# Inverse window transform of a fused attention and filter kernel: half of the third tile's columns are computed on the other half of the partitions, in a fourth accumulator bank

## The chip, the cores and the metric

The kernel runs on one core of one Trainium2 chip. The metric is device time in microseconds (us) of one execution. The time before is the median of three executions. One execution was also taken with the hardware profiler, and all durations below come from that one.

The engines are called by the profile's names. PE is the matrix engine (TensorE), with its weight loads shown apart as PEld. DVE is VectorE, ACT is ScalarE, POOL is GpSimd and SP issues most of the transfers. An accumulator bank (PSUM) holds 512 fp32 numbers on each of 128 partitions. PE writes only there, and ACT or DVE copy from there to the working memory (SBUF).

## The reference, cut to what matters

The input is 8 images of 384 channels and 64 x 64 pixels, all fp32. There are two layers, each added to its input:

```
x = x + windowed attention(group norm(x))
x = x + second layer(group norm(x))

second layer:
  t  = w_in @ x                                  # 384 channels to 384, each pixel alone
  tf = rfft2 of every 8 x 8 window of t          # "P = 8"
  t  = irfft2(tf * fft_filter)                   # back to pixels
  t  = 3 x 3 depthwise convolution of t          # zero padding at the image's edge
  g  = gelu(t[:192], exact) * t[192:]
  out = w_out @ g                                # 192 channels to 384
```

The change lies in the line with `irfft2`. A real 8 x 8 window has 64 numbers, and the kernel does its transform as a product with a 64 x 64 matrix.

## The kernel before, in words

An image is cut into 8 strips of 8 rows. A strip has 8 windows of 64 pixels, so 512 pixels, and 384 channels, so three tiles of 128 channels x 512 pixels. The second layer's hidden channels are permuted so that tile 0 and tile 1 go together into the gate (`gelu(tile 0) * tile 1`), while tile 2 holds the last 64 channels of both halves.

The work is a list of pieces. Each piece is put at a place in time with `at(place, piece, ...)` (lines 848 to 947), and the pieces are then traced in the order of their places (line 953). PE's instructions stay in exactly that order (`keep_in_program_order`, line 62). A scheduler orders the instructions of the other engines by its own estimate of when their inputs are ready. The second layer of one image runs in the same stretch of time as the attention layer of the next, so that seven eighths of the kernel is one steady mixture; the second layer of the last image runs alone.

Two units of places make a strip. In the second unit of each strip the pieces that matter here come on PE in this order, with the names that the profile shows:

- `v_tile` (line 490): the attention's values for the next image's strip, accumulated in `pvv` twice; ACT copies each to `v` at line 503. Between the two stands `turn` (line 551, tile `pT`), a transpose of attention weights.
- `back` (line 684): the inverse transform. The filtered spectrum is in two tiles `t2`, each for four windows, whose 128 partitions are two halves of 64 frequencies; which half holds which channels is told by the index `h`. Each matmul takes 64 channels of one window (`t2` as the stationary matrix, 64 x 64) and the 64 x 64 basis `inv`, and leaves 64 channels x 64 pixels in an accumulator `pz`. The row half of the PE array is `h`, the column half is the half of the partitions of `pz` that is written.
- `apply` (line 562, tile `pA`): attention weights times values, 32 matmuls of 64 x 64 that go round all four quarters of the PE array.
- `scores` (line 505, tile `pS`): the next strip's attention scores, also 64 x 64 blocks.
- `finish` (line 810): the last product of an older strip of the second layer. It first multiplies 64 rows of `g1` into two banks `pw` and then into the double bank `pw2`, and then does dense 128 x 128 matmuls with `zz` (the profile's `pw<-zz`).
- `qk_tile`, `project` and `mix` follow, which are dense 128 x 128 matmuls.

On ACT, `inner` (line 702) copies a tile from `pz` to a bordered image tile `z` of 10 x 66, from which DVE later does the convolution. `back` calls it for tiles 0 and 2; `borders` (line 713) calls it for tile 1 and then copies border rows between neighbouring strips (lines 718 and 719). `put` (line 587) copies `pA` into `o` with four copies on ACT at lines 602 to 605, or two at line 599, and POOL then issues transfers from `o` to `oT` (line 615). The square at line 376 (`sq<-y`) and the first tap at line 779 come next on ACT.

There are eight accumulator banks. Four single banks take turns under the tag `gemm` (`ps`, `bufs=4`): each new tile takes the bank of the tile four allocations earlier and waits until that one has been read. The other four banks are two double banks under the tag `att` (line 55), which `pT`, `pA`, `pS` and `pw2` take in turn. So `pw2` takes the double bank of `pA` and can be written only when `put` has copied `pA`.

In `back` the first group of matmuls fills tiles 0 and 2, with four matmuls for each window, one for each quarter of the PE array. The second group fills tile 1, with two matmuls for each window on two opposite quarters. An fp32 matmul is two passes in the profile, so the groups have 64 and 32 passes.

The table `EMPTY` (line 29) tells how many empty instructions are spread over PE's dense matmuls ahead of each stretch of small ones. `small_tiles` marks those stretches.

Of the kernel before, what the change touches and what calls it, by code (L numbers as in the profile page):

```python
# [8 lines left out]
AF = mybir.ActivationFunctionType  # L9
# [3 lines left out]
P = 128  # L13
KC = 3
C = 384
WS = 8
SW = 64
ST = WS * SW
NS = SW // WS
# [6 lines left out]
C_ID, C_ONES, C_GRP, C_FWD, C_INV, C_MASK = 0, 128, 256, 384, 512, 640  # L26
C_PICK = C_MASK + 3 * 64
N_CONST = C_PICK + 2
EMPTY = (129, 0, 0, 96, 52, 0, 0, 98, 11, 124, 11, 124, 3, 124, 11, 124, 11, 45, 43, 124, 52, 123, 11, 124,
# [9 lines left out]
def block_kernel(ctx: ExitStack, tc: tile.TileContext, out, x, consts, fsel, wqk, wv, bqk, bv,  # L39
                 wp, bp, lng, lnb, rpb1, rpb2, w_in, w_dw, w_out, filt):  # L40
    nc = tc.nc
# [8 lines left out]
    def psum(name):  # L50
        return ps.tile([P, ST], F32, tag="gemm", name=name)
# [9 lines left out]
    def matmul(*args, **kw):  # L61
        tc.keep_in_program_order(nc.tensor.matmul(*args, **kw))  # L62

        n = min(fetched["empty"], fetched["share"])
        for _ in range(n):
            tc.keep_in_program_order(nc.tensor.nop(hint="empty"))
        fetched["empty"] -= n
# [28 lines left out]
    inv = cst[:, C_INV:C_INV + P]  # L96
# [71 lines left out]
    for br, tab in ((0, rpb1), (1, rpb2)):  # L168
        raw = sb.tile([P, 2, 64], F32, tag="t2", bufs=3, name=f"rpb_raw{br}")
        raw_bias.append(raw)  # L170
        for h in range(4):
            half = slice(h % 2 * 64, h % 2 * 64 + 64)
# [117 lines left out]
    def by_window(t):  # L290

        return t.rearrange("p (w r c) -> p w r c", w=NS, r=WS)
# [10 lines left out]
    xs, ys, y2s, qks, vs, os_, ots, x1s, zs = ({} for _ in range(9))  # L303
# [380 lines left out]
    def back(b, s):  # L684

        t2 = [zs.pop((b, s, "t2", j)) for j in range(2)]
        pz = [psum(f"pz_{b}_{s}_{m}") for m in (0, 2, 1)]
        pz = {0: pz[0], 2: pz[1], 1: pz[2]}

        for parts in (((0, 0, 0, 0), (2, 1, 1, 128), (0, 1, 0, 64), (2, 0, 1, 64)),  # L690
                      ((1, 0, 0, 128), (1, 1, 1, 0))):
            for i in range(4):
                for p in range(2):
                    for m, half, h, c in parts:
                        rows = slice(h * 64, (h + 1) * 64)
                        matmul(pz[m][half * 64:(half + 1) * 64, (2 * i + p) * 64:(2 * i + p + 1) * 64],
                               t2[i // 2][rows, p, i % 2, c:c + 64], inv[rows, rows], start=True, stop=True)
        zs[b, s, "pz"] = pz
        for m in (0, 2):
            inner(b, s, m)  # L700

    def inner(b, s, m):
        z = z_bufs[zs["count"] % len(z_bufs)]
        zs["count"] += 1
        if s == 0:
            nc.gpsimd.memset(z[:, 0, 1:SW + 1], 0.0)
        if s == NS - 1:
            nc.gpsimd.memset(z[:, WS + 1, 1:SW + 1], 0.0)
        nc.scalar.activation(z[:, 1:9, 1:SW + 1].rearrange("p r (w c) -> p w r c", c=WS),
                             by_window(zs[b, s, "pz"][m]), AF.Copy)  # L710
        zs[b, s, m] = z

    def borders(b, s):

        inner(b, s, 1)
        for m in (0, 2, 1) if s else ():
            above, z = zs[b, s - 1, m], zs[b, s, m]
            after_out(nc.scalar.copy(above[:, WS + 1, 1:SW + 1], z[:, 1, 1:SW + 1]))  # L718
            after_out(nc.scalar.copy(z[:, 0, 1:SW + 1], above[:, WS, 1:SW + 1]))
# [128 lines left out]
    for b in range(B):  # L848
# [25 lines left out]
        for s in range(NS):  # L874
# [18 lines left out]
            for br in range(2):  # L893
                w = u + br
# [27 lines left out]
        for s in range(NS):  # L922
            u = first + 2 + 2 * s
            at(u - 0.84, load, b, s, "mix")
            at(u + 0.02, normal_x1, b, s)
            for i in range(4):
                at(u + (0.28, 0.45, 0.60, 0.78)[i], mix, b, s, i)
            for j in range(2):
                at(u + (0.995, 1.02)[j], transform, b, s, j)
            if b < B - 1:  # L930
                at(u + 1.985, small_tiles, u + 2)
            at(u + 1.99, back, b, s)
            at(u + 2.08 if b < B - 1 or s < NS - 1 else u + 1.991, borders, b, s)

            for n, m in enumerate((0, 2, 1)):
                for tap in range(1, 6):
                    at(u + (2.62, 3.10, 3.5)[n] + 0.05 * tap + (0.4 if n == 2 and tap > 3 else 0), conv, b, s, m, tap)
                for tap in range(6, 9):
                    at(u + 4.2 + 0.25 * (n * 3 + tap - 6) / 9, conv, b, s, m, tap)
            if (b, s) in on_pool:  # L940
                for place, taps in ((2.45, (0, 1)), (2.8, (2, 3)), (3.15, (4, 5)), (4.15, (6, 7)), (4.3, (8,))):
                    at(u + place, pool_taps, b, s, taps)
            if (b, s) in on_pe:
                at(u + 2.3, conv_taps, b, s)
            at(u + 5.16, load, b, s, "finish")
            at(u + 4.5, gate, b, s)
            at(u + 6.10, finish, b, s)
# [5 lines left out]
    order = [p[2:] for p in sorted(plan, key=lambda p: p[:2])]  # L953
    dense, empty, counts = [], [0] * len(order), list(EMPTY)
    for i, (piece, args) in enumerate(order):
# [116 lines left out]
```

## Time and profile before

| what | value |
|---|---|
| median of 3 executions | 3534.49 us (3533.04 to 3534.71) |
| the profiled execution | 3528.99 us, span of its instructions 3526.8 us |
| mean granted PE clock | 0.992 |
| PE busy | 3450.3 us (98%) |
| DVE busy | 3062.2 us (87%) |
| ACT busy | 2535.8 us (72%) |
| POOL busy | 1055.3 us (30%) |
| `pz` matmuls | 6144 passes, 146.7 us busy |
| copies of `pz` to `z` (line 709) | 192 of 128x512, 656 ns each |

The profiled execution took 5.5 us (0.16%) less than the median of the three others. Its span is 2.2 us shorter than its own time. A matmul's row shows 218 ns for a pass of 64 columns though a new one begins every few ns, because matmuls overlap; the chain of waits counts that overlap only once. In rows of the timeline, equal instructions that follow each other are merged: `x3` after a duration means that three instructions took that long together.

### The profile page before, as it was taken

The page shows a single profiled execution, that of the slowest core. Times are in us where ns is not written, and L with a number is a line of the kernel's source. Part 1 is how long each engine was busy: PE and PEld are TensorE (multiplying, and loading weights), DVE is VectorE, ACT ScalarE, POOL GpSimd, SP SyncE. Part 2 cuts the span into 40 slices and gives each one's busy share as a digit, 9 for nine tenths or more (in the row PEclk, how much of TensorE's full clock was granted, in tenths as well). Part 3 has the DMA queues.
Part 4 walks back from the last instruction along what each step waited for, and adds up shares of the span by engine and source line. Part 5 has one row for each costly group of instructions (what it writes and reads, how often), then busy time and mean ns, then how long its engine had stood idle before and what let it go on. Part 6 is the DMA issues. An engine that isn't in the chain of part 4 may idle for free.

```text
span 3526.8 us, 93350 instructions
## 1 busy us (share of the span) xinstructions
PE 3450.3 (98%) x36454; PEld 2192.9 (62%) x36454; DVE 3062.2 (87%) x4330; ACT 2535.8 (72%) x4069; POOL 1055.3 (30%) x1688
## 2 busy tenths in 40 slices
PE   7999999999999999999999999999999999999888
PEld 5666666666666666666666666666666666666554
DVE  5676589889998899998999889998899988987987
ACT  5877777768777687776777767777777767776574
POOL 6433222323222232222233223232232223222244
PEclk8999999999999999999999999999999999999999
DMA  4343234323343334333344324433234333323432
GB/s 135 117 128 100 88 119 138 107 101 133 130 148 108 117 107 153 120 121 109 119 136 140 119 89 141 138 116 133 101 118 156 113 107 109 108 99 104 160 109 81
DMA packets 176101, 421.13 MB, mean 119 GB/s; under 512 B 26656, under 2 KB 29243, under 8 KB 175688
## 3 DMA queue, kind: packets, MB, share of 16 engines
q1 hardware_dynamic: 138832, 364.25, 29.6%
q0 software_dynamic: 36416, 50.65, 5.1%
q8 instruction: 316, 5.18, 0.6%
q14 instruction: 97, 0.79, 0.1%
q10 hardware_dynamic: 440, 0.27, 0.0%
HBM read 263.92 MB, written 100.79 MB: 103 GB/s over the span
## 4 chain that ended last, share of the span: by engine, by line
PE 87%; DVE 8%; ACT 2%; issue 1%; DMA 1%; POOL 0%; SPq 0%; ACTq 0%; POOLq 0%; DVEq 0%
PE pq L62 26%; PE pr L62 14%; PE pvv L62 13%; PE pt L62 11%; PE pw L62 6%; PE pA L62 3%; PE pz L62 3%; PE pT L70 3%; PE pS L62 3%; DVE zz L785 2%; PE pf L62 2%; DVE acc L785 1%; PE ln L62 1%; DVE t L681 1%; ACT tap L753 1%
## 5 line engine op out<-in xcount | busy, mean ns | idle before, releaser
L785 DVE SCALAR_TENSOR_TENSOR zz<-z,dw_sb,zz 128x512 f32<-128x512 f32 x1331 | 1026.5, 797 | 10.8
L62 PE MATMUL pq<-y,wqk_sb 128*128 128x512 f32 x2160 | 989.4, 597 | 0.9 <-ACT kcd L470 0.7
L615 POOL DMA_DIRECT2D oT<-o x960 | 480.2, 508 | 963.4 <-ACT z L718 431.2
L62 PEld LDWEIGHTS pq<-y,wqk_sb 128*128 128x128 f32 x2160 | 403.1, 190 | 448.0 <-issue 407.3
L62 PE MATMUL pt<-wi_sb,xn 128*128 128x384 f32 x1536 | 535.1, 487 | 3.0 <-ACT xn L654 3.0
L62 PE MATMUL pr<-oT,wp_sb 128*128 128x512 f32 x1152 | 523.9, 593 | 1.6 <-DMA oT<-o 1.6
L62 PE MATMUL pvv<-wv_sb,y 128*128 128x192 f32 x2880 | 507.4, 326 | 0.0
L62 PEld LDWEIGHTS pvv<-wv_sb,y 128*128 128x128 f32 x2880 | 471.7, 190 | 48.6 <-issue 33.7
L62 PEld LDWEIGHTS pt<-wi_sb,xn 128*128 128x128 f32 x1536 | 290.9, 191 | 232.8 <-issue 74.1
L452 POOL COPY y<-y 128x384 f32<-128x384 f32 x112 | 86.0, 768 | 1108.0 <-PE pvv L62 643.7
L62 PEld LDWEIGHTS pr<-oT,wp_sb 128*128 128x128 f32 x1152 | 217.5, 190 | 263.7 <-issue 246.3
L470 ACT ACTIVATE kcd<-pq,bqk_sb 32x512 f32<-32x512 f32 x512 | 348.4, 680 | 9.1
L470 ACT ACTIVATE qab<-pq,bq_sb,cst 96x512 f32<-96x512 f32 (+1 forms) x256 | 197.7, 772 | 181.1 <-PE pq L62 178.7
L503 ACT COPY v<-pvv 128x384 f32<-128x384 f32 x256 | 121.4, 474 | 191.5 <-PE pvv L62 190.0
L470 ACT ACTIVATE kab<-pq,bqk_sb 96x512 f32<-96x512 f32 (+1 forms) x256 | 174.1, 680 | 90.4 <-PE pq L62 86.1
L470 ACT ACTIVATE qcd<-pq,bq_sb,cst 96x512 f32<-96x512 f32 (+1 forms) x256 | 197.4, 771 | 33.5 <-PE pq L62 27.7
L382 POOL TENSOR_TENSOR sq<-sq 128x512 f32<-128x512 f32 x122 | 201.4, 1651 | 5.8
L537 DVE TENSOR_TENSOR e<-e,mx 128x1024 f32<-128x1024 f32 x128 | 199.3, 1557 | 3.9
L530 DVE TENSOR_TENSOR e<-pS,bias 128x512 f32<-128x512 f32 (+2 forms) x200 | 108.1, 547 | 93.9 <-PE pS L62 93.9
L547 DVE TENSOR_REDUCE rc<-e 128x16 f32<-128x1024 f32 x128 | 155.1, 1211 | 35.2 <-ACT e L542 35.1
L62 PE MATMUL pw<-zz,wo_sb 128*128 128x512 f32 x496 | 182.2, 509 | 0.0
L625 DVE SCALAR_TENSOR_TENSOR x_add<-pr,vec,x_add 128x512 f32<-128x512 f32 x192 | 142.6, 743 | 38.9 <-PE pr L62 38.2
(166 smaller groups left out, 5376.3 us busy)
## 6 DMA issues: line engine op xcount, KB each, us to landing
x_add<-in_x_dram SPq DMA_DIRECT2D x64, 768.0 KB
x1d<-x_add SPq DMA_DIRECT2D x64, 768.0 KB
x_finish<-x1d SPq DMA_DIRECT2D x64, 768.0 KB
out_dram<-x_finish SPq DMA_DIRECT2D x64, 768.0 KB
x_norm<-in_x_dram SPq DMA_DIRECT2D x61, 768.0 KB
x_stats<-in_x_dram SPq DMA_DIRECT2D x56, 768.0 KB
x_mix<-x1d SPq DMA_DIRECT2D x56, 768.0 KB
oT<-o POOLq DMA_DIRECT2D x192, 96.0 KB, 3.7
```

The source lines that it names most:

```text
L62: tc.keep_in_program_order(nc.tensor.matmul(*args, **kw))
L70: tc.keep_in_program_order(nc.tensor.transpose(*args, **kw))
L382: nc.gpsimd.tensor_tensor(sq[:, 0, :], sq[:, 0, :], sq[:, k, :], ALU.add)
L452: nc.gpsimd.tensor_copy(dst[:, :, :, :, 0:4], src[:, :, :, :, 4:8])
L470: return nc.scalar.activation(dst[to:to + n], pq[of:of + n], AF.Identity, bias=bias[of:of + n], scale=scale)
L503: nc.scalar.copy(v[:, 384 * g:384 * (g + 1)], pvv[:, 0:384])
L530: nc.vector.tensor_tensor(e5[:, odd, :, a:z, :], pS[:, odd, :, a:z, :], bias_t[br, kind, odd].unsqueeze(2).to_broadcast([P, 2, z - a, 64]) ...
L537: zs["soft"] = nc.vector.tensor_tensor(e, e, mx.unsqueeze(2).to_broadcast([P, 2 * NS, 64]), ALU.subtract)
L547: nc.vector.tensor_reduce(rc, e, AX.X, ALU.add)
L615: nc.gpsimd.dma_start(out=oT[to % P:to % P + z - a, to // P, rows], in_=o[row + a:row + z, h // 2, of:of + n])
L625: after_softmax(nc.vector.scalar_tensor_tensor(t[:, m, :], pr, bp_sb[:, m:m + 1], t[:, m, :], ALU.add, ALU.add))
L785: i = nc.vector.scalar_tensor_tensor(acc.rearrange("p (r c) -> p r c", c=SW), z[:, dy:dy + 8, dx:dx + SW], dw_sb[:, m, TAPS[tap]:TAPS[tap] ...
```

## The change

`back` asks for a fourth bank, `pz_turned`. Tile 1 is now made in four windows' worth of steps instead of eight. In each step, the two matmuls as before make one of the first four windows in the bank of tile 1, and two more matmuls, on the two other quarters of the PE array, make one of the last four windows in the bank `turned`. Because those quarters have row and column halves crossed, the channels of the last four windows lie on the wrong half of the partitions. The number of matmuls stays the same.

`inner` for tile 1 then makes three copies on ACT in place of one: 128 partitions x 256 pixels from the bank of tile 1, and two of 64 partitions x 256 pixels from the bank `turned`, each going to the other half of the partitions. Tiles 0 and 2 are copied as before. One number in `EMPTY` goes from 98 to 96.

```diff
-        pz = [psum(f"pz_{b}_{s}_{m}") for m in (0, 2, 1)]
-        pz = {0: pz[0], 2: pz[1], 1: pz[2]}
+        pz = {m: psum(f"pz_{b}_{s}_{m}") for m in (0, 2, 1, "turned")}
 
         for parts in (((0, 0, 0, 0), (2, 1, 1, 128), (0, 1, 0, 64), (2, 0, 1, 64)),
-                      ((1, 0, 0, 128), (1, 1, 1, 0))):
-            for i in range(4):
-                for p in range(2):
-                    for m, half, h, c in parts:
-                        rows = slice(h * 64, (h + 1) * 64)
-                        matmul(pz[m][half * 64:(half + 1) * 64, (2 * i + p) * 64:(2 * i + p + 1) * 64],
-                               t2[i // 2][rows, p, i % 2, c:c + 64], inv[rows, rows], start=True, stop=True)
+                      ((1, 0, 0, 128), (1, 1, 1, 0), ("turned", 1, 0, 128), ("turned", 0, 1, 0))):
+            for w in range(NS if parts[0][0] == 0 else NS // 2):
+                for m, half, h, c in parts:
+                    rows, to = slice(h * 64, (h + 1) * 64), w + (NS // 2 if m == "turned" else 0)
+                    matmul(pz[m][half * 64:(half + 1) * 64, to * 64:(to + 1) * 64],
+                           t2[to // 4][rows, to % 2, to // 2 % 2, c:c + 64], inv[rows, rows], start=True, stop=True)
...
-        nc.scalar.activation(z[:, 1:9, 1:SW + 1].rearrange("p r (w c) -> p w r c", c=WS),
-                             by_window(zs[b, s, "pz"][m]), AF.Copy)
+        whole, half = slice(0, P), SW // 2
+        for m_, to, of, w in ((m, whole, whole, 0),) if m != 1 else (
+                (1, whole, whole, 0), ("turned", slice(0, 64), slice(64, P), 1), ("turned", slice(64, P), slice(0, 64), 1)):
+            cols = slice(1 + w * half, 1 + half + w * half) if m == 1 else slice(1, SW + 1)
+            tok = slice(w * ST // 2, (w + 1) * ST // 2) if m == 1 else slice(0, ST)
+            nc.scalar.activation(z[to, 1:9, cols].rearrange("p r (w c) -> p w r c", c=WS),
+                                 zs[b, s, "pz"][m_][of, tok].rearrange("p (w r c) -> p w r c", r=WS, c=WS), AF.Copy)
```

More of the change, by code (lines that the diff above doesn't have):

```diff
@@ L28 @@
 N_CONST = C_PICK + 2
-EMPTY = (129, 0, 0, 96, 52, 0, 0, 98, 11, 124, 11, 124, 3, 124, 11, 124, 11, 45, 43, 124, 52, 123, 11, 124,
+EMPTY = (129, 0, 0, 96, 52, 0, 0, 96, 11, 124, 11, 124, 3, 124, 11, 124, 11, 45, 43, 124, 52, 123, 11, 124,
          11, 124, 11, 124, 3, 124, 11, 124, 11, 45, 43, 124, 52, 123, 11, 124, 11, 124, 11, 124, 3, 124, 11, 124,
```

## The prediction

> **What bounds the kernel now.** I read the page first, its busy shares and its chain.
>
> ```profile
> PE 3450.3 (98%) x36454; PEld 2192.9 (62%) x36454; DVE 3062.2 (87%) x4330; ACT 2535.8 (72%) x4069; POOL 1055.3 (30%) x1688
> ...
> PE 87%; DVE 8%; ACT 2%; issue 1%; DMA 1%; POOL 0%; SPq 0%; ACTq 0%; POOLq 0%; DVEq 0%
> ```
>
> PE sets the time nearly everywhere, so time saved on PE counts unless PE then waits. The chain around one regular inverse transform (strip 4 of image 2, at 1492.85 us) shows what it costs. Columns: start, us, what.
>
> ```profile
> 1492.92 1.95 PE pz L62 x94
> ...
> 1494.93 0.93 PE pA L62 x61
> 1495.86 0.94 PE pS L62 x49
> 1496.79 4.07 PE pw L62 x20
> ```
>
> The 96 passes of `pz` take 1.95 us, while `pA`, 64 passes on all four quarters, takes about 0.93 us. The starts of single matmuls in the trace agree: a step begins every 58 ns, with four passes in the first group and two in the second. So each group is 16 steps, 0.93 us.
>
> Next I asked whom PE waits for: first its weight loads, then its matmuls (total us, times, longest).
>
> ```profile
> PEld pw L62 <- ACT o L605: 40.4, 51, 2.7
> ```
>
> ```profile
> PE pw L62 <- ACT o L605: 10.7, 10, 1.8
> ```
>
> In 51 of 56 strips the last thing that `pw2`'s weights wait for is ACT's last copy of `pA`. Only ten times does this stop PE itself, since the `pw` matmuls before it still run. The rows below show how near it is: the ACT timeline of the regular strip, then its weight loads.
>
> ```profile
> 1494.06 1.72 ACT L709 ACTIVATE z<-pz 128x512 f32<-128x512 f32 x3 [0.62 <-PE pz L62]
> 1495.99 0.59 ACT L602 COPY o<-pA 128x512 f32<-128x512 f32 x1 [0.21 <-PE pA L62]
> 1496.47 0.49 ACT L603 COPY o<-pA 128x384 f32<-128x384 f32 x1
> 1496.84 0.23 ACT L604 COPY o<-pA 128x64 f32<-128x64 f32 x1
> 1496.94 0.24 ACT L605 COPY o<-pA 128x64 f32<-128x64 f32 x1
> ```
>
> ```profile
> 1497.24 0.39 PEld L62 LDWEIGHTS pw<-g,wo_sb 64*64 64x64 f32 x8 [0.47 <-ACT o L605]
> 1498.02 0.30 PEld L62 LDWEIGHTS pw<-zz,wo_sb 128*128 128x128 f32 x2 [0.39 <-issue]
> ```
>
> ACT ends L605 at 1497.18, the weights go at 1497.24, and the dense `pw<-zz` begins 0.84 us after L605. In strip 7 of the same image, PE did stop:
>
> ```profile
> 1663.70 0.64 ACT L709 ACTIVATE z<-pz 128x512 f32<-128x512 f32 x1
> 1664.22 0.56 ACT L602 COPY o<-pA 128x512 f32<-128x512 f32 x1
> ...
> 1665.15 0.23 ACT L605 COPY o<-pA 128x64 f32<-128x64 f32 x1
> ```
>
> ```profile
> 1665.43 0.66 PE L62 MATMUL pw<-g,wo_sb 64*64 64x256 f32 x8 [0.85 <-ACT o L605]
> 1666.03 1.55 PE L62 MATMUL pw<-zz,wo_sb 128*128 128x512 f32 x3
> ```
>
> There `pw<-zz` comes 1666.03 - 1665.38 = 0.65 us after L605. In a regular strip, then, PE can arrive at most 0.84 - 0.65 = 0.19 us earlier before ACT's `put` holds it.
>
> **Saved on PE.** The second group's 16 steps become 8, because four quarters work at once as in the first group: 8 x 58 ns = 0.47 us for each of 64 strips, 29.9 us in all. The number of matmuls stays.
>
> **Added on ACT.** One copy of 128x512 becomes three 256 wide. The three merged copies took 1.72 us, one takes 0.656, so they start (1.72 - 0.66) / 2 = 0.53 us apart. The step by width is (0.48 - 0.10) / (512 - 64) = 0.85 ns per element, from the starts of L602 to L605. A 256-wide copy thus takes 0.53 - 256 x 0.85 ns = 0.31 us, start to start; three take 0.93, or +0.40 us a strip. No row shows one with crossed partitions. The bounds are 0.10 us (the 64-wide copy) and 0.53 (the 512-wide); worked through the steps below they give -19 and +35 us in all. I take 0.31, since the 64-, 384- and 512-wide rows lie on one line. A half of the partitions saves nothing: the Gelu rows are 629 ns with 64 partitions and 630 with 128.
>
> **The path in a regular strip.** `pz` of tile 0 is ready as before, so tile 1's copies start as before, at 1494.06 + 2 x 0.53 = 1495.12. The pieces end at 1495.12 + 0.93 = 1496.05. PE ends `pA` 0.47 us earlier, at about 1495.4, so `put` now waits for ACT instead of PE: it starts at 1496.05 against 1495.99. L605 ends at 1497.24, `pw<-zz` starts at 1497.89 against 1498.02. Of 0.47 us saved only about 0.12 arrives. About 36 strips are like this (strips 1 to 6 of most images): -4.3 us.
>
> **Where ACT is already the bound.** In the first strip of images 1 to 6 the normalisation copies of the next strip (L654) push `pz`'s copies back; in the last strip of images 0 to 5 three of them stand before tile 1's copy; and in two strips of image 6 the tap matrices (L732) do. PE waits for L605 there, so +0.40 us each goes on the path: 14 x 0.40 = +5.6 us.
>
> **The added wait.** The fourth bank was `v_tile`'s second one, so the crossed matmuls wait for its copy at L503, and `apply`, `scores` and `pw` are queued behind them. In a regular strip L503 ends 0.59 us after `pz` begins and the crossed matmuls come at 0.93, so this is hidden with 0.34 us to spare. Without that cover every us of a late L503 would stop PE. It is late in the first strips (2.63 us after the start in image 0), where ACT's queue hides it again, but image 0 has no `finish` yet, so there the second group ends 2.68 + 0.45 = 3.13 instead of 1.87: +1.3 us, once. In last strips the bank is that of the deviation at L283 (ready 2.05 us after the start, with a table load): PE stops about 1.1 us, inside the wait for L605 and a gap of 1.0 us at `pA` that it already has.
>
> **The rest.** Strip 1 of image 0, without `finish`, keeps its 0.47 us: -0.5. In the last image PE waits for DVE (17.8 us at `pz`); the tile is ready 0.47 us earlier and copied 0.40 later: 0, within 1 us either way. Behind the copies on ACT stand the border rows, L376, L779 and POOL's transfers to `oT`, all about 0.06 us later in a regular strip; PE waited for `oT` once, 1.6 us. With that cover gone, 0.06 x 56 is 3.4 us. No queue of SP or POOL changes. Two empty instructions fewer: 0; misplaced ones would show as "issue" at small matmuls, where PE now loses 5.9 us in all.
>
> **The sum.** -4.3 + 5.6 + 1.3 - 0.5 = +2.1 us. The profiled execution was 3528.99 us and would become 3531.1; the median of the runs lies 5.5 higher, so 3534.5 + 2.1 = 3536.6 us.
>
> **A rule against this change.** The row is PE's wait for L605, 51 times. The Trainium skill's page "TensorEngine Tiling (Array Packing)", section "PSUM Bottleneck", says that tiling quickens the matrix engine but not the emptying of the accumulators, whose copy may become the bottleneck. Taken at its word nothing saved on PE arrives, and the sum would lose its two negative terms, +6.9 us; the rows leave 0.12 us a strip.
>
> **The rivals.** *The saving arrives* (faster). ACT's order is the scheduler's, which put tile 1's copy ahead of `put` though it stands behind it in the program. If `put` went ahead of the turned copies, it would start at 1495.5, and L605 would no longer hold PE: 36 x -0.47 = -17 us, or -30 if all 64 strips gain; the middle is 3511 us. For it: the program's order. Against: tile 1's copy ran before `put` in every strip of images 0 to 6, and all three pieces are ready together, before `pA`.
>
> *The copies cost more than I think* (slower), on ACT between `pz` and `put`. At 0.35 us each, `pw<-zz` of a regular strip is where it was; above that each strip loses. If the pieces did not overlap, each costs 0.656 - 0.22 = 0.44 us: 3 x 0.13 - 0.12 = +0.27 us in 36 strips, 0.79 in 14: 9.7 + 11.1 + 0.8 = +22 us, 3556 us. For it: new forms, and two banks to wait for. Against: the present copies overlap by 0.13 us.
>
> *It does not do what it says*: crossed quarters into two banks run two at a time. Then PE saves nothing, and +5.6 remains with up to +3 for the late L376: 3540 to 3543. Against: the first group writes two banks in just this way.
>
> **How the numbers follow.** A measurement of this kernel tells a change from none at about 0.2%, 7 us. The forecast (+2.1, its own range -5 to +9 for scheduler shifts) gets 0.55, the saving 0.17, dear copies 0.20, no saving 0.08. Within 0.2%: most of the forecast and some of the last, 0.50. Faster: the saving and an edge of the forecast, 0.17. Slower: dear copies, an edge of the forecast and half of the last, 0.33. The range 3517 to 3557 leaves out the greater part of the saving's case and the top of the dear copies.
>
> **What would show it.** Right: `pz` 0.47 us shorter in the chain; three copies 0.31 us apart; L602 starting back to back with them and no longer waiting for `pA`; matmul waits of `pw` for L605 growing from 10 to some 50 times, near 30 us in all. The forecast is wrong if L602 still waits for `pA`, if `pz` waits for L503 in regular strips, or if new issue gaps appear.

## The result, and the profile after

The changed kernel took 3549.02 us (median of 6 executions, 3547.29 to 3554.18), the kernel before 3532.91 us beside it (6 executions, 3529.52 to 3534.71). The ratio is 1.005, with a 95% interval of 1.004 to 1.0059: the change costs about 16 us. The profiled execution took 3547.29 us, its span 3545.5.

The page of the changed kernel, busy shares and chain:

```profile
PE 3439.3 (97%) x36454; PEld 2162.4 (61%) x36454; DVE 3063.6 (86%) x4330; ACT 2577.0 (73%) x4197; POOL 1056.6 (30%) x1688
...
PE 87%; ACT 7%; DVE 3%; DMA 2%; issue 1%; POOL 0%; SPq 0%; ACTq 0%; POOLq 0%; DVEq 0%
```

PE is busy 11 us less and the kernel is longer: ACT's share of the chain went from 2% to 7%. The regular strip that the prediction used (strip 4 of image 2) now starts at 1498.99 us. Its chain of waits (start, us, what):

```profile
1500.62 0.98 PE pA L62 x63
...
1501.69 0.41 ACT z L712
1502.12 0.42 ACT z L712
...
1503.80 3.44 PE pw L62 x16
```

`pA` starts 1.63 us after the first `pz` where it started 2.08 us after it, so the 0.45 us were saved on PE. But from 1501.6 on the chain has left PE: it runs over the copies of `z`, then over the copies of `pA`, to `pw`. The ACT timeline of this strip, then its weight loads:

```profile
1500.20 1.48 ACT L712 ACTIVATE z<-pz 128x512 f32<-128x512 f32 x3 [0.63 <-PE pz L62]
1501.69 0.83 ACT L712 ACTIVATE z<-pz_turned 64x256 f32<-64x256 f32 x2
1502.55 0.58 ACT L602 COPY o<-pA 128x512 f32<-128x512 f32 x1
...
1503.50 0.24 ACT L605 COPY o<-pA 128x64 f32<-128x64 f32 x1
```

```profile
1503.80 0.21 PEld L62 LDWEIGHTS pw<-g,wo_sb 64*64 64x64 f32 x8 [1.34 <-ACT o L605]
1504.39 0.30 PEld L62 LDWEIGHTS pw<-zz,wo_sb 128*128 128x128 f32 x2 [0.39 <-issue]
```

Two turned copies take 0.83 us with a gap and no overlap, and L602 starts only after the second has ended. The starts of single copies in the trace are 0.424 us apart from tile 1's first copy on (1501.27, 1501.69, 1502.12, 1502.55). L605 ends at 1503.74, and `pw<-zz` comes 0.65 us later, as the prediction had said of a strip that ACT holds. Counted from the first `pz`, it is at 5.40 us, against 5.17 before: 0.23 us later in each such strip.

PE's own waits (total us, times, longest), and those of its weight loads:

```profile
PE pw L62 <- ACT o L605: 34.5, 51, 2.1
...
PE pz_turned L62 <- ACT v L503: 5.8, 7, 1.4
PE pz_turned L62 <- ACT sd_b L283: 5.0, 6, 0.8
```

```profile
PEld pw L62 <- ACT o L605: 79.6, 52, 3.0
```

The strips show where the time went. A strip's period is the time from its first `pz` to that of the next. The table gives the sum of its changes against the kernel before, in us, from one profiled execution of each kernel; the last two columns are runs told of below.

| strips | forecast | changed kernel | x5_no_crossing | x3b_put_ahead_even |
|---|---|---|---|---|
| 37 regular (forecast: 36) | -4.3 | +8.8 | -16.9 | -16.9 |
| first strips of images 1 to 6 | +2.4 | +4.5 | +1.4 | -0.8 |
| last strips of images 0 to 5 | +2.4 | +3.1 | +0.3 | -3.1 |
| two with tap matrices | +0.8 | +1.5 | +0.1 | -1.1 |
| strips 0 and 1 of image 0 | +0.8 | +1.6 | +1.3 | +2.3 |
| the rest, to the first `pz` of the last strip | 0 | +1.5 | +0.2 | +3.7 |

In the regular strips the period changes by nearly the same amount every time (+0.22 to +0.26 us in 36 of the 37; strip 6 of image 0 has +0.14), so this row is no noise. The start, up to the first `pz`, came 1.6 us earlier here and lay between 2.7 us earlier and 1.7 later in kernels in which nothing there was touched.

### The profile page after: what moved, and what is told of

It is laid out like the page before. It is cut to its first block, busy times and chain, and to the rows that moved or that the text cites. A ratio compares the mean times of both kernels' runs of the same rounds, so it can differ in the third digit from the quotient of the medians.

```text
span 3545.5 us, 93486 instructions
## 1 busy us (share of the span) xinstructions
PE 3439.3 (97%) x36454; PEld 2162.4 (61%) x36454; DVE 3063.6 (86%) x4330; ACT 2577.0 (73%) x4197; POOL 1056.6 (30%) x1688
## 4 chain that ended last, share of the span: by engine, by line
PE 87%; ACT 7%; DVE 3%; DMA 2%; issue 1%; POOL 0%; SPq 0%; ACTq 0%; POOLq 0%; DVEq 0%
PE pq L62 27%; PE pr L62 14%; PE pvv L62 13%; PE pt L62 12%; PE pw L62 6%; PE pA L62 3%; PE pT L70 3%; PE pf L62 2%; PE pz L62 2%; PE pS L62 2%; ACT z L712 2%; PE ln L62 1%; DMA x_mix<-x1d 1%; ACT o L602 1%; DVE acc L788 1%
## 5 line engine op out<-in xcount | busy, mean ns | idle before, releaser
L470 ACT ACTIVATE kcd<-pq,bqk_sb 32x512 f32<-32x512 f32 x512 | 348.4, 680 | 9.1
L470 ACT ACTIVATE qab<-pq,bq_sb,cst 96x512 f32<-96x512 f32 (+1 forms) x256 | 197.6, 772 | 180.5 <-PE pq L62 178.1
L503 ACT COPY v<-pvv 128x384 f32<-128x384 f32 x256 | 121.4, 474 | 181.7 <-PE pvv L62 180.1
L470 ACT ACTIVATE kab<-pq,bqk_sb 96x512 f32<-96x512 f32 (+1 forms) x256 | 174.1, 680 | 87.1 <-PE pq L62 83.4
L470 ACT ACTIVATE qcd<-pq,bq_sb,cst 96x512 f32<-96x512 f32 (+1 forms) x256 | 197.4, 771 | 32.6 <-PE pq L62 27.2
L838 DVE TENSOR_TENSOR x_finish<-pw,x_finish 128x512 f32<-128x512 f32 x128 | 87.6, 690 | 102.6 <-PE pw L62 102.5
```

The costliest lines, as they stand in the source:

```text
L470: return nc.scalar.activation(dst[to:to + n], pq[of:of + n], AF.Identity, bias=bias[of:of + n], scale=scale)
L503: nc.scalar.copy(v[:, 384 * g:384 * (g + 1)], pvv[:, 0:384])
L838: nc.vector.tensor_tensor(t[:, m, :], pw[m][0], t[:, m, :], ALU.add)
```

## The experiments

The theory after the result was: PE's saving is there, but three copies, each followed by the next after 0.424 us, stand ahead of the copies of `pA`, and `pw2` waits for those. Three things were open: whether the turned copies are dear because they cross partitions or because they use 64 partitions; whether getting `put` past them brings the saving; and whether the fourth bank costs anything by itself.

### Copies alone: three straight parts, two straight parts

Both kernels leave PE as it was before and only cut tile 1's copy. The diff is that of x1; in x2 the last two parts are one, `(slice(0, P), 4, 4)`.

```diff
-        nc.scalar.activation(z[:, 1:9, 1:SW + 1].rearrange("p r (w c) -> p w r c", c=WS),
-                             by_window(zs[b, s, "pz"][m]), AF.Copy)
+        for rows, w, n in ((slice(0, P), 0, NS),) if m != 1 else ((slice(0, P), 0, 4), (slice(0, 64), 4, 4), (slice(64, P), 4, 4)):
+            cols, tok = slice(1 + w * WS, 1 + (w + n) * WS), slice(w * 64, (w + n) * 64)
+            nc.scalar.activation(z[rows, 1:9, cols].rearrange("p r (w c) -> p w r c", c=WS),
+                                 zs[b, s, "pz"][m][rows, tok].rearrange("p (w r c) -> p w r c", r=WS, c=WS), AF.Copy)
```

> The kernel before with one edit: tile 1's copy by ScalarE is cut into three (all partitions and the left half of the columns, then the lower 64 partitions and the upper 64 partitions of the right half), each from its own partitions; TensorE's part and the banks stay as before. Theory 1 (a copy over 64 partitions costs ScalarE about 0.425 us from its start to the next one's start, whether partitions are crossed or not): ScalarE comes to the copies of pA 0.42 us later, of which 0.19 us is slack in a regular strip: 38 x 0.23 + 14 x 0.42 = about +15 us, 3548 us. Theory 2 (the crossing alone is what takes the overlap of two copies away): starts 0.31 us apart, the regular strips unchanged, 14 x 0.40 = about +6 us, 3539 us. Theory 3 (the copies are harmless, the loss of the changed kernel comes from its fourth bank and its order on TensorE): within 2 us of the kernel before.

> The kernel before with tile 1's copy cut into two of 128 partitions x 256 columns each, TensorE as before. Theories 1 and 2 (a copy over all partitions onto the same partitions overlaps with the one ahead of it): starts about 0.31 us apart, ScalarE +0.1 us per strip, below the 0.19 us of slack in a regular strip: 0 to +2 us, 3533 to 3535 us. Rival (a short copy does not overlap, whatever its partitions): starts 0.42 us apart, +0.3 us per strip: 38 x 0.1 + 14 x 0.3 = about +8 us, 3541 us.

x1 took 3544.19 us against 3532.12 (ratio 1.0033, 1.002 to 1.0045), x2 3531.22 (0.9998, 0.9989 to 1.0007). In the regular strips x1 is 0.06 to 0.10 us longer in 36 of 37, and x2 unchanged. In x1's profiled execution the regular strips cost 2.7 us, the 14 others 4.7 and the rest, mostly the last image, 5.3; why the last image lost so much stays open. The ACT timeline of x1 in the same strip:

```profile
1493.67 2.17 ACT L711 ACTIVATE z<-pz 128x512 f32<-128x512 f32 x5 [0.63 <-PE pz L62]
1495.86 0.59 ACT L602 COPY o<-pA 128x512 f32<-128x512 f32 x1
```

The five copies and L602 start 0.54, 0.52, 0.27, 0.43 and 0.44 us apart. x2's two halves and L602 start 0.27 us apart where nothing else is waited for: a 256-wide copy in the manner of the copies before costs 0.27 us, less than the forecast's 0.31. In x1 the first 64-partition copy still overlaps with the one ahead of it (0.27 us); the second, on the upper 64 partitions, does not, and L602 after it does not either. So neither theory was right. The crossing alone is not the cause, since nothing crosses in x1 and two of its distances are 0.43 us all the same; the 64 partitions are not it either, since one 64-partition copy overlaps. What the separated ones have in common is that the partition at which a copy starts is another than that of the copy ahead.

### Which partitions

x7 is the changed kernel with more and shorter copies. Each entry of its list gives a bank, the partitions written, the partitions read, the first window and the number of windows.

```diff
+        whole, low, up = slice(0, P), slice(0, 64), slice(64, P)
+        for m_, to, of, w, n in {0: ((0, whole, whole, 0, 8),),
+                                 2: ((2, whole, whole, 0, 4), (2, low, low, 4, 2), (2, low, low, 6, 2),
+                                     (2, up, up, 4, 2), (2, up, up, 6, 2)),
+                                 1: ((1, whole, whole, 0, 4), ("turned", low, up, 4, 2), ("turned", low, up, 6, 2),
+                                     ("turned", up, low, 4, 2), ("turned", up, low, 6, 2))}[m]:
 ...
```

> A look at distances alone: in the changed kernel, tile 2's copy in five (128 partitions x 256, then lower 64, lower 64, upper 64, upper 64 partitions x 128, all straight) and the turned bank in four (upper to lower twice, lower to upper twice, 64 x 128 each). A copy of 128 columns takes about 0.30 us by itself. Theory A (a copy overlaps with the one ahead only when both start on the same partitions, at the source and at the target): the second of each like pair starts about 0.17 us after the first, the others 0.31 us. Theory B (any copy that moves between partitions is kept apart): the straight pairs 0.17 us, all turned ones 0.31 us. Theory C (a copy over 64 partitions is kept apart from the next, wherever it lies): all 0.31 us but the first lower one. The time of the whole is above that of the changed kernel by the added copies.

The kernel took 3590.34 us; only its distances were wanted. The ACT timeline of a regular strip, at the turned bank:

```profile
1515.29 0.91 ACT L714 ACTIVATE z<-pz_turned 64x128 f32<-64x128 f32 x4
1516.22 0.58 ACT L602 COPY o<-pA 128x512 f32<-128x512 f32 x1
```

Four copies of 0.27 to 0.29 us take 0.91 together. Their starts are 0.178, 0.291 and 0.175 us apart: the second of a like pair overlaps, although it crosses partitions, and the change from one pair to the other takes the overlap away. The straight 64-partition copies do the same: 0.15 us (lower, lower), 0.30 (lower, upper), 0.18 (upper, upper), while the step from 128 partitions to the lower 64 took 0.27 us for a copy that lasts 0.41. For the copies of `pz`, theory A holds in all 64 strips: one overlaps with the one ahead only if both start on the same partitions, where they read and where they write. In the changed kernel the start changes at three steps, from tile 1's first copy to the first turned one, from there to the second and from there to L602, so each of these loses its 0.14 us or so.

The trace of the kernel before had rows that pointed this way: the copies at L470, among them some that move 32 partitions elsewhere (the first `kab` copy, of 96 partitions, stays where it is, and the second moves). The ACT timeline of before, some 12 us ahead of the regular strip:

```profile
1480.29 1.37 ACT L470 ACTIVATE kab<-pq,bqk_sb 96x512 f32<-96x512 f32 x2 [1.69 <-PE pq L62]
1481.67 1.37 ACT L470 ACTIVATE kcd<-pq,bqk_sb 32x512 f32<-32x512 f32 x2
```

Two copies of 0.68 us take 1.37: back to back, with no overlap. By themselves these rows do not prove the rule: the first `kab` copy starts on partition 0 like the copy at L664, and it too began only 0.025 us after the end of one, 24 times.

### The turned bank without the crossing

x5 leaves out the move between the halves of the partitions, so the last four windows of tile 1 get their channels in exchanged halves.

```diff
-                (1, whole, whole, 0), ("turned", slice(0, 64), slice(64, P), 1), ("turned", slice(64, P), slice(0, 64), 1)):
+                (1, whole, whole, 0), ("turned", whole, whole, 1)):
```

> The changed kernel with the second bank copied by one instruction over all 128 partitions, straight (so tile 1's right half of the columns gets its two halves of channels in each other's place; TensorE's part is that of the changed kernel). Theory 1 (the loss comes from copies that do not overlap with the one ahead of them since they start on other partitions): starts 0.27 us apart as in x2_straight_halves, the copies of pA start 2.28 + 2 x 0.27 = 2.83 us after the first pz, 0.31 us ahead of the kernel before, and TensorE's 0.45 us arrive in nearly all regular strips: 38 x 0.35 to 0.45, the 14 others -0.3 each, less 1 to 2 us for the wait in the first strips: 15 to 20 us below the kernel before, about 3515 us. Rival (ScalarE's copies cost no more than their time beside TensorE, the fourth bank or its order is what loses): 3540 to 3549 us.

It took 3513.16 us against 3532.24: ratio 0.9943, 0.9929 to 0.9956, 19 us below the kernel before. The ACT timeline of the regular strip (first `pz` at 1486.28):

```profile
1487.49 1.48 ACT L712 ACTIVATE z<-pz 128x512 f32<-128x512 f32 x3 [0.62 <-PE pz L62]
1488.83 0.43 ACT L712 ACTIVATE z<-pz_turned 128x256 f32<-128x256 f32 x1
1489.11 0.61 ACT L602 COPY o<-pA 128x512 f32<-128x512 f32 x1
```

L602 starts 2.83 us after the first `pz`, as expected, and 36 of the 37 regular strips are 0.45 or 0.46 us shorter, the other 0.55. PE's part, the fourth bank and the order are those of the changed kernel. So the loss lies in the two crossed copies in place of one straight one, and PE's saving arrives in full as soon as ACT lets it. The 14 other strips did not gain the 0.3 us each that was expected: first strips lost 0.2 each on average (from 0.1 gained to 0.46 lost), the last ones and those with the tap matrices 0.07 or less. The fourth bank by itself shows in strip 0 of image 0, 1.3 us longer here too.

### `put` ahead of tile 1's copies

```diff
+            i = nc.scalar.activation(z[to, 1:9, cols]..., zs[b, s, "pz"][m_][of, tok]..., AF.Copy)
+            if m == 1:
+                after_out(i)
```

`after_out` puts an instruction behind the last copy of `pA`. x3 does this in the changed kernel, x4 in the kernel before.

> The changed kernel with tile 1's three copies put behind the copies of pA in ScalarE's queue. Theory 1 (the changed kernel loses because three copies stand ahead of the copies of pA that TensorE waits for): with them out of the way TensorE's 0.45 us per strip arrive in most of the 64 strips, 38 to 50 x 0.45: 17 to 22 us below the kernel before, 3511 to 3516 us; TensorE's waits for the last copy of pA fall from some 50 long ones to some 10. Rival (ScalarE as a whole is the next bound, its 1.3 us of copies only move behind the copies of pA and hold up the exponentials or the next strip's copies instead): 3528 to 3545 us, with the waits on other lines of ScalarE. Rival (the fourth bank is what costs): no gain over the changed kernel, 3549 us.

> The kernel before with tile 1's one copy put behind the copies of pA in ScalarE's queue: what the order alone is worth, without the turned bank. All theories: the regular strips are held by TensorE's own work, so nothing there; up to 14 strips that ScalarE held gain up to 0.5 us each: 0 to -7 us, about 3529 us. If it gained 17 us or more, the gain of the run with the changed kernel's order would be the order's and not the turned bank's.

x4 took 3526.04 us against 3532.12 (0.9981, 0.9972 to 0.999): regular strips unchanged, 5.2 us gained in the 14 others, as expected. x3 took 3547.75 us (1.0046, 1.0033 to 1.0058), 16 us above the kernel before, far from the expected 3511 to 3516. PE's waits for L605 had gone (2.3 us in 3 waits). Up to strip 11 or so (counted from 0 over all images) the regular strips were 0.45 us or more shorter, each of them; from strip 14 on they were 0.02 to 1.4 us longer than before. The PE timeline of x3 in strip 1 of image 4 (strip 33 of the 64, first `pz` at 2185.91 us):

```profile
2189.22 1.03 PE L62 MATMUL pw<-g,wo_sb 64*64 64x512 f32 x7
2191.19 1.02 PE L62 MATMUL pw<-g,wo_sb 64*64 64x512 f32 x9 [0.93 <-issue]
```

PE stands still for 0.93 us in the middle of `pw`, and the row names no engine. The row of the weight loads behind the stop, at 2191.28, names a border copy (L723), but that one ended at 2191.22, when the stop was over. In the early strips the same order cost nothing. What differs along the kernel is where a strip's instructions lie in PE's stream. In the trace a strip has 1280 of them from `pz` to `pz`, give or take two, in the kernel before and in the changed one (weight loads, passes, waits and empty ones). In x3 most strips have 1281: tile 1's copies now come after those of `pA`, and PE has 49 waiting instructions more, 859 against the 810 of the changed kernel. Counting from the first instruction, in the order of their starts, every stop of 0.03 us or more at `pw` in x3's regular strips lies at 193 or 194 within a run of 256. The first weight loads of `pw2` had moved from 178 in strip 14 to 189 in strip 26 and 210 in strip 50; in the kernel before they lie at 166 in every regular strip.

```diff
-EMPTY = (129, 0, 0, 96, 52, 0, 0, 96, 11, 124, 11, 124, 3, 124, 11, 124, 11, 45, 43, 124, 52, 123, 11, 124,
+EMPTY = (129, 0, 0, 96, 52, 0, 0, 94, 11, 123, 11, 123, 3, 123, 11, 124, 11, 44, 43, 123, 52, 122, 11, 123,
 ...
```

> The run with the copies of pA ahead (x3_put_ahead) once more, with 46 of its empty instructions on TensorE taken out, one for each waiting instruction that its order had added on TensorE, so that each strip again has as many TensorE instructions as in the kernel before (1280). Theory 1 (x3_put_ahead brought 0.45 us in each of the regular strips 2 to 12 and lost it from strip 13 on because one instruction more per strip moved TensorE's stream against its blocks, which shows as 'issue' ahead of pw): the regular strips keep -0.45 us to the end, the 14 others gain up to 0.5 us: 38 x 0.45 + some 5 = 20 to 24 us below the kernel before, 3508 to 3513 us; TensorE's issue waits at pw back from 130.8 to some 97 us. Rival (the late copies of tile 1 hold up the strips from 13 on, by the banks or by the convolution): the later strips stay 0.2 to 1.4 us longer, 3540 to 3548 us.

(49 empty instructions were taken out in the end.) It took 3510.79 us against 3532.24: ratio 0.9938, 0.9925 to 0.995, 21 us below the kernel before. The issue waits of the weight loads of `pw`, in x3 and then in x3b:

```profile
PEld pw L62 <- issue: 130.8, 389, 1.9
```

```profile
PEld pw L62 <- issue: 96.6, 333, 1.9
```

PE's own stops at `pw` with no engine named, 13.7 us in 26 waits in x3, are gone, and those put down to tile 1's copies (L712) fell from 3.4 us to 0.6 though the order is the same. The first weight loads of `pw2` lie at 166 again in every regular strip.

The ACT timeline of the regular strip in x3b (first `pz` at 1487.52):

```profile
1490.19 0.58 ACT L602 COPY o<-pA 128x512 f32<-128x512 f32 x1 [0.27 <-ACT z L712]
...
1491.15 0.24 ACT L605 COPY o<-pA 128x64 f32<-128x64 f32 x1
1491.25 0.46 ACT L712 ACTIVATE z<-pz 128x256 f32<-128x256 f32 x1
1491.74 0.83 ACT L712 ACTIVATE z<-pz_turned 64x256 f32<-64x256 f32 x2
```

L602 now starts as soon as `pA` is done (1.63 + 0.98 us), 2.67 us after the first `pz` against 3.14 before (the releaser that the row names had ended 0.27 us earlier). The dear copies are still there, 0.49 and 0.42 us apart, but behind L605, and all 37 regular strips keep at least 0.45 us. x3 and x3b differ in the empty instructions alone, and that is worth 37 us. With x4 beside it, some 6 us of x3b's 21 are the order's and the other 15 need the turned bank. x3b is the fastest of the kernels run, ahead of both the kernel before and the changed one.

## Why the prediction came out as it did

The forecast was 3536.6 us, no measurable change; the time was 3549.02, inside the range but slower by 0.5%, where the forecast had put 0.33. The sum was some 14 us short, and only the width of the range held the time. The rival "the copies cost more than I think" came true, with its own mechanism and nearly its own price: 0.44 us for each copy against 0.424 measured, and +22 us against +18.7 in the profiled spans (16 by the medians).

- **Saved on PE.** Right: 0.45 us a strip against 0.47, and the quarters do work four at a time.
- **Added on ACT.** This is the step that failed. The forecast took 0.31 us for a copy, from widths of copies that all start on partition 0. The three copies cost 0.424 us each, and L602 came 0.42 us later against the 0.06 of the forecast. The sentence that no row showed a copy with crossed partitions was wrong: the rows of L470 did, and the two copies of `kab` stand back to back in all 128 pairs. So did the Gelu row with 64 partitions that the prediction quotes: L804 reads the lower half of the partitions and writes the upper. The choice of 0.31 "since the rows lie on one line" took a law for the width and used it for another variable, the partitions.
- **The path in a regular strip.** The arithmetic was right, its input was not: with 0.424 it gives 3 x 0.424 - 0.93 = 0.34 us later than forecast, so -0.12 + 0.34 = +0.22, and +0.24 was measured. The slack of 0.19 us and the 0.65 us from L605 to `pw<-zz` both held to 0.01 us, in x1 as well (0.27 - 0.19 = 0.08).
- **Where ACT is already the bound.** The 14 strips were named rightly and cost +9.2 us instead of +5.6. In the last strips ACT's order put `put` between the two turned copies, so that only two copies stood ahead: +0.35 us in five of six.
- **The added wait.** Right: hidden in regular strips, 1.28 us in strip 0 of image 0 against 1.3. PE waited 5.8 us at L503 and 5.0 at L283 in all, 13 times.
- **The rest.** Strip 1 of image 0 lost 0.28 us where 0.47 were to be gained: PE already stood still for 0.38 us at `pS` in this strip, and stands 1.16 us now, with no engine named. In both kernels this stop lies at 193 or 194 of 256, like those of x3; what PE waits for there stays open. Two empty instructions fewer left the changed kernel's strips at 1280 instructions and `pw2` at 166; what they cost was not tried by itself. The sentence named the sign of misplaced ones, issue waits at small matmuls, but not that one instruction a strip can decide 37 us, as in x3 and x3b.
- **A rule against this change.** The Trainium skill's page "TensorEngine Tiling (Array Packing)", section "PSUM Bottleneck", named the place where the loss arose: the copies out of the accumulators. Its figure by the rule, +6.9 us, was still too small, because the copying out did not stay as it was but became dearer.
- **The saving arrives.** The rival's middle of 3511 us is what x3b measured, 3510.79, by the order that it described. That they agree to 0.2 us is luck: the rival put the middle between a gain in 36 strips and one in all 64, while x3b gained 16.9 us in the 37 regular strips and 5.0 in the 14 where ACT was the bound, and lost 2.3 in strips 0 and 1 of image 0. It did not come by itself: the scheduler kept tile 1's copies ahead, as the argument against it had said.
- **What would show it.** Most of the signs were met, among them L605 waits 51 times, 34.5 us in all, and L602 back to back. They told the forecast from its faster rival, but not from the dearer copies; only the distance of the copies did.

## What to carry to other kernels

Price an added copy by a row that is like it in every respect that the engine could see, the partitions at both ends too, and take the start-to-start distance of such copies, not their duration. Ask of each piece of time that is saved on the bound engine who is next: here the answer was 0.19 us away, and the saving arrived when the copies that PE waits for went ahead of the new ones (x3b), or when the new ones cost less (x5, without the move that the result needs). After any change of order, compare the count of the bound engine's instructions per period, waits included.

## What the runs showed of the hardware that was not expected

- **Whether ScalarE's copies of `pz` overlap depends on where the partitions start.** Copies of `pz` that start on the same partitions as the one ahead, and L602 behind them, overlapped by 0.11 to 0.17 us; after a change of the start, at the source or the target, the next began 0.01 to 0.03 us after the end of the last. This is no rule for all pairs. In x1's last image the first tap (L781), which starts on partition 0, seven times began 0.11 us before the end of the copy on the upper 64 partitions. In the kernel before, L718 began 0.02 us after the end of L605 in 33 of 48 strips, though both start on partition 0, and overlapped by 0.12 to 0.15 us in the others. What decides there was not tried. The Trainium skill's page "ScalarE: Activation LUTs", section "What ACT_TABLE_LOAD costs", says that back-to-back instructions overlap by about 93 ns; for like starts the rows come near it (0.094 us between the copies at L654, 0.11 to 0.15 between those of `pz`), after a change of start they do not.
- **Stops of PE at one place in 256 instructions.** The stops at `pw` in x3's regular strips lay at 193 or 194 of 256, for 0.03 to 0.95 us each, and a strip of 1280 instructions is five times 256. The stops at `pA` that the kernel before has in eight first and last strips (0.08 to 1.0 us) lie there too. The Trainium skill's page "Runtime: NRT & Kernel Launch", section "Instruction fetch mechanics", says that instructions are fetched in blocks of 256 and that crossing from one to the next is mostly hidden. The distance of 256 agrees. If the fetch is what PE waits for, it is not hidden at these places, where the matmuls and weight loads just ahead (64 columns) start every few ns. That the fetch is the cause was not tried by itself; the profile says only "issue".
- **A wait is an instruction.** One more waiting instruction in most strips moved PE's stream by one place a strip and cost 37 us over x3b, which has the same waits and as many empty instructions fewer.
